# What is left of the earlier blocks in a layer's last step: done before or after the last block's scores

## The chip, the cores and the metric

The kernel runs on one core of one Trainium2 chip. The metric is the device time in microseconds (us) of one launch. Five engines work side by side, each through its own list of instructions: TensorE (PE in the profile; its weight loads are PEld), VectorE (DVE), ScalarE (ACT), GpSimd (POOL) and SyncE (SP), which here only issues transfers.

## The reference

Four layers of graph attention over the same 4096 nodes of 256 features. Each layer normalises x row by row, applies a relu, lets every node attend to its neighbours in `adj` (some eight of the 4096, and itself), and adds the result to x. Cut to what matters:

```python
# layers 0 to 2, with their own weights and slopes
h = relu(layernorm(x))
Wh = h @ W                                       # 4 heads of 64; one head of 256 in layer 1
e = leaky_relu(s_i[:, None] + s_j[None, :])      # s_i, s_j: one number a node and head
alpha = softmax(where(adj == 0, -inf, e), axis=1)
x = x + act(alpha @ Wh)                          # elu in layer 0; layer 1 returns Wh + alpha @ h
# layer 3
q, k, v = h @ Wq + bq, h @ Wk + bk, h @ Wv + bv  # 4 heads of 64
scores = q @ k.T / 8 + (adj.T - 1) * 10000
x = x + softmax(scores) @ v
```

## The kernel before

The first part of the kernel (some 400 us) turns `adj` into a list of neighbours for each node, sorts the nodes by their number of neighbours and writes them to DRAM in that order. It is not touched. After it the nodes lie in 32 blocks of 128, one node to a partition; a block needs as many gathers as its fullest node has neighbours (`CAPS`, 23 down to 3, and six fewer in layer 0). `ORDER` takes the blocks from both ends, 0, 31, 1, 30, and so on; the last four are 14, 17, 15 and 16, with 9, 8, 8 and 8 gathers. In the text they are w, x, y and z.

`layer(l)` (line 806 on) runs one layer. Each layer has a table in DRAM, one row to a node: its features, and the numbers its scores need; in layer 3 keys and values. A block goes through these stages:

- `fill`: GpSimd gathers one row per neighbour from the layer's table into `s_ring` (L755), up to four blocks ahead, as room in the ring allows. In layer 3 SyncE also loads the block's own values (L831).
- `scores`: VectorE and ScalarE work out the softmax's exponentials. In layers 0 to 2 these are small instructions over the gathered numbers (L912 to L945, the exp at L952). In layer 3 VectorE multiplies all gathered keys by the query and sums them (L932, L935, up to eight rows at a time), after a copy of the query by ScalarE (L927).
- `weigh`: VectorE divides by the sum (L987 to L989), multiplies the block's own row (L1014) and the gathered rows by their shares (L1028), and TensorE sums the rows in PSUM by matmuls with the identity (L1019, L1021, L1033, L1038).
- `settle`, in two parts: part 0 is ScalarE's exp for the elu, in layer 0 alone (L1052, L1053). Part 1 adds the sum to x and starts the next layer's normalisation (L1063 to L1067, statistics at L569 and L570, ScalarE at L575 and L577). In layer 3 it only makes the output block (L1057, L1058).
- `norm`: VectorE ends the normalisation (L579 to L585), ScalarE scales and applies the relu (L732), TensorE turns the block (L740). Empty in layer 3.
- `product`: ScalarE copies the turned block (L742), TensorE multiplies it by the next layer's weights (L748). Empty in layer 3.
- `third`: VectorE adds what is to be added to the product (L1080, or L1094 to L1104) and the row is sent to the next layer's table, by GpSimd after layer 0 (L765) and by SyncE after layers 1 and 2 (L1088, L1095). It also sends all that waits in `made`, in layer 3 the output blocks (L765).

Everything in the layers is issued in program order: an engine's list is what the Python loop writes. The loop is a pipeline over the blocks. With S = 2 and N = 3 (layers 0, 2 and 3) step i takes the scores and the weighing of block i, settles block i - 2, and does norm and product of block i - 3 and the third stage of block i - 4. Layer 1 has S = 0 and N = 1. After the last step a tail finishes what is left, by hand. The first gather of the next layer needs its whole table, so the last row that the tail writes.

In the profile DVE L1094 is thus third, L1067 settle, L579 norm, L932 or L913 the scores, L987 to L1028 weighing.

Of the kernel before, what the change touches and what calls it, by code (L numbers as in the profile page):

```python
# [50 lines left out]
ORDER = [b for k in range(16) for b in (k, 31 - k)]  # L51
# [18 lines left out]
class Sparse:  # L70
# [735 lines left out]
    def layer(self, l):  # L806


        nc, nt, vs = self.nc, self.nt, {}
        wide = (W, WL, W, 2 * D)[l]  # L810
        slots = RING // wide
        ring = self.ring[:, : slots * wide].rearrange("p (k w) -> p k w", w=wide)
        todo, held, at = list(ORDER), {}, 0
        made = []

        def fill(i):
            nonlocal at
            while todo and nt - len(todo) <= i + AHEAD:
                j = todo[0]
                K = self.slots(l, j)  # L820

                room = K + (K % 2 if l > 1 else 0)
                s = (at if at + room <= slots else 0) if K else 0
                if any(s < e and b < s + room for b, e in held.values()) or (
                    l == 3 and len(held) > 3
                ):
                    return
                todo.pop(0)
                if l == 3:
                    vs[j] = self.pool.tile([P, D], F32, name=f"s_vself_{j}", tag="vself", bufs=5)  # L830
                    nc.sync.dma_start(out=vs[j], in_=self.tab[3][ts(j, P), D:])  # L831
                k0 = EARLY if l == 0 else 0
                for k in range(K):
                    at_k = self.near[:, j, k0 + k : k0 + k + 1]
                    self.fetch(ring[:, s + k, :], self.tab[l], at_k)
                held[j] = (s, s + room)
                at = s + room if K else at

        sums, behind, turning, rows = {}, {}, {}, {}

        def settle(c, parts=(0, 1)):

            if 0 in parts and c in sums:
                behind[c] = self.settle(l, c, sums.pop(c), made)
                next(behind[c])
            if 1 in parts and c in behind:
                next(behind[c])

        def norm(d):

            if l < 3 and d in behind:
                turning[d] = self.turned(self.pool, next(behind.pop(d)), f"{l + 1}_{d}")
                next(turning[d])

        def product(d):
            if d in turning:
                rows[d] = self.advance(l + 1, d, next(turning.pop(d)), made)
                next(rows[d])

        def third(d):  # L860
            if d in rows:
                next(rows.pop(d), None)
            for send in made:
                self.send(*send)
            made.clear()

        S, N = (0, 1) if l == 1 else (2, 3)
        for i in range(nt):
            fill(i)
            b, c, d, e = (ORDER[k] if k >= 0 else None for k in (i, i - S, i - N, i - N - 1))  # L870
            if S:
                settle(c, (0,))
            norm(d)
            g = ring[:, held[b][0] : held[b][1], :]
            p = self.scores(l, b, self.rows[b], g[:, : self.slots(l, b), :])
            third(e)
            if S:
                settle(c, (1,))
            product(d)
            sums[b] = self.weigh(l, b, vs.pop(b) if l == 3 else self.rows[b][:, 0:D], g, p)  # L880
            del held[b]
            if not S:
                settle(b)
        z, y, x, w = ORDER[-1:-5:-1]
        if S:
            settle(y)
            norm(x)
            third(w)
            product(x)
            settle(z)  # L890
            norm(y)
            third(x)
            product(y)
        norm(z)
        third(y)
        product(z)
        third(z)

    def scores(self, l, b, mine, g):

# [775 lines left out]
```

## Time and profile before

| | us |
|---|---|
| median of three runs | 1838.98 (1837.8 to 1839.6) |
| span of the profiled execution | 1839.6 (1841.3 with what lies around it) |
| VectorE busy | 1379.9 (75%) |
| GpSimd busy | 1184.8 (64%) |
| TensorE busy, matmuls | 994.8 (54%) |
| ScalarE busy | 423.7 (23%) |
| first gather of layer 1, issued at | 658.8 |
| last table write of layer 2, issued at | 1409.6 |
| first gather of layer 3, issued at | 1412.4 |
| last output block, issued at | 1834.0 |

The profile is one execution. Its page gives each engine's busy time, the granted TensorE clock (mean 0.751 of full speed here), the chain that ended last, and groups of instructions; the trace behind it gives every instruction with its start, its duration and what ended the idle time before it. A busy share is a mean over stages with different limits, so a change at a layer's end is read in the timeline of that end.

### The profile page before, as it was taken

The page shows a single profiled execution, that of the slowest core. Times are in us where ns is not written, and L with a number is a line of the kernel's source. Part 1 is how long each engine was busy: PE and PEld are TensorE (multiplying, and loading weights), DVE is VectorE, ACT ScalarE, POOL GpSimd, SP SyncE. Part 2 cuts the span into 40 slices and gives each one's busy share as a digit, 9 for nine tenths or more (in the row PEclk, how much of TensorE's full clock was granted, in tenths as well). Part 3 has the DMA queues.
Part 4 walks back from the last instruction along what each step waited for, and adds up shares of the span by engine and source line. Part 5 has one row for each costly group of instructions (what it writes and reads, how often), then busy time and mean ns, then how long its engine had stood idle before and what let it go on. Part 6 is the DMA issues. An engine that isn't in the chain of part 4 may idle for free. (4 is left out here: it accounts for less than half of the span.)

```text
span 1839.6 us, 14362 instructions
## 1 busy us (share of the span) xinstructions
PE 994.8 (54%) x2569; PEld 481.7 (26%) x2569; DVE 1379.9 (75%) x3900; ACT 423.7 (23%) x1240; POOL 1184.8 (64%) x1324
## 2 busy tenths in 40 slices
PE   4878787750666611222232167788785344565555
PEld 3523232220455400111111023343342111221122
DVE  6899989850688808888888257888885587887777
ACT  5864435000244401111111002222222000000000
POOL 1067756676566357777776477777772577776774
PEclk9988889875788855555555588889987676777777
DMA  9899877348533134444444344444443577666763
GB/s 319 281 394 363 287 259 254 97 148 242 168 87 88 51 84 128 131 132 130 132 132 121 69 111 133 134 135 131 136 131 97 156 215 210 208 208 181 209 205 108
DMA packets 123017, 312.89 MB, mean 170 GB/s; under 512 B 31236, under 2 KB 49671, under 8 KB 122920
## 3 DMA queue, kind: packets, MB, share of 16 engines
q0 software_dynamic: 68064, 207.46, 39.7%
q1 hardware_dynamic: 54856, 104.44, 16.2%
q14 instruction: 73, 0.60, 0.1%
q8 instruction: 24, 0.39, 0.1%
HBM read 276.80 MB, written 35.00 MB: 169 GB/s over the span
## 5 line engine op out<-in xcount | busy, mean ns | idle before, releaser
L755 POOL DMA_INDIRECT s_ring<-s_tab,s_near x924 | 883.8, 956 | 356.7 <-issue 190.4
L1033 PE MATMUL s_acc<-s_ring,s_ident 128*128 128x512 f32 x588 | 319.5, 697 | 183.3 <-issue 95.0
L1033 PEld LDWEIGHTS s_acc<-s_ring,s_ident 128*128 128x128 f32 x588 | 130.5, 228 | 368.2 <-issue 245.5
L755 POOL DMA_INDIRECT s_g<-s_tab,s_keep x192 | 183.2, 954 | 64.3 <-issue 57.0
L483 DVE MAX8 s_cand<-s_pt 128x8 f32<-128x256 f32 x512 | 181.6, 417 | 16.4 <-PE s_pt L481 15.9
L1028 DVE TENSOR_TENSOR s_ring<-s_ring,s_shares 128x2048 f32<-128x2048 f32 (+7 forms) x121 | 187.5, 1573 | 0.0
L740 PE MATMUL s_pht<-s_ident,s_h 128*128 128x128 f32 x128 | 34.3, 361 | 248.0 <-ACT s_h L732 248.0
L748 PE MATMUL s_ps<-s_we_l,s_ht 128*128 128x264 f32 x256 | 113.4, 586 | 79.2 <-ACT s_ht L742 79.2
L999 DVE SCALAR_TENSOR_TENSOR s_acc<-s_ring,s_p,s_acc 128x256 f32<-128x256 f32 x277 | 135.7, 490 | 9.7
L261 ACT ACTIVATE s_low<-s_raw 128x1024 fp8e4<-128x1024 int32 x128 | 134.2, 1050 | 21.3 <-DMA s_raw<-in_adj_dram 18.1
L556 PE MATMUL s_ae<-s_g,s_ident 128*128 128x512 f32 x192 | 113.7, 688 | 36.5 <-DVE s_g L547 36.5
L913 DVE TENSOR_TENSOR s_e<-s_ring,s_rx 128x8 f32<-128x8 f32 (+12 forms) x87 | 15.7, 181 | 148.0 <-DMA s_ring<-s_tab,s_near 143.0
L476 PE MATMUL s_pt<-s_low,s_mark 128*128 128x512 fp8e4 x256 | 107.7, 421 | 34.3 <-DVE s_cand L483 15.0
L748 PE MATMUL s_ps_kv<-s_wkv,s_ht 128*128 128x512 f32 x128 | 82.9, 782 | 73.6 <-ACT s_ht L742 73.6
L932 DVE TENSOR_TENSOR s_ring<-s_ring,s_shares 128x2048 f32<-128x2048 f32 (+7 forms) x48 | 81.1, 1690 | 47.8 <-DMA s_ring<-s_tab,s_near 31.5
L481 PE MATMUL s_pt<-s_places,s_stands 128*128 128x512 bf16 x256 | 106.5, 416 | 1.4 <-DVE s_stands L453 1.4
L952 ACT ACTIVATE s_shares<-s_e 128x32 f32<-128x32 f32 (+8 forms) x87 | 17.4, 200 | 387.8 <-DVE s_e L945 340.2
L575 ACT ACTIVATE s_y<-s_mv,s_eps 128x1 f32<-128x1 f32 x96 | 28.3, 294 | 294.0 <-DVE s_mv L570 294.0
L740 PEld LDWEIGHTS s_pht<-s_ident,s_h 128*128 128x128 f32 x128 | 18.3, 172 | 287.9 <-ACT s_h L732 271.9
L748 PEld LDWEIGHTS s_ps<-s_we_l,s_ht 128*128 128x128 f32 x256 | 63.0, 272 | 110.0 <-ACT s_ht L742 100.1
L935 DVE TENSOR_REDUCE s_e<-s_ring 128x32 f32<-128x2048 f32 (+7 forms) x48 | 81.2, 1692 | 1.7
L1021 PE MATMUL s_acc<-s_me,s_ident 128*128 128x512 f32 x60 | 42.8, 803 | 70.8 <-DVE s_me L1014 67.2
(193 smaller groups left out, 1673.4 us busy)
## 6 DMA issues: line engine op xcount, KB each, us to landing
s_raw<-in_adj_dram SPq DMA_DIRECT2D x128, 512.0 KB, 7.8
s_ring<-s_tab,s_near POOLq DMA_INDIRECT x924, 3.0
s_rx<-s_placed SPq DMA_DIRECT2D x32, 262.0 KB, 8.0
s_tab<-s_kv SPq DMA_DIRECT2D x32, 256.0 KB, 2.8
s_tab<-s_keep SPq DMA_DIRECT2D x8, 528.0 KB, 6.8
s_tab<-s_rx SPq DMA_DIRECT2D x32, 132.0 KB, 2.3
s_keep<-in_x_dram SPq DMA_DIRECT2D x8, 512.0 KB, 4.1
s_vself<-s_tab SPq DMA_DIRECT2D x32, 128.0 KB, 2.9
```

What stands on the lines that cost most here:

```text
L261: nc.scalar.activation(low[r][:, ts(h, n // 4)], raw.pop(q), AF.Copy, saturate=False, accum_out=self.sums[:, r, h : h + 1],)
L476: nc.tensor.matmul(pt, lhsT=self.mark, rhs=lo[:, ts(g, IB)], start=True, stop=False)
L481: nc.tensor.matmul(pt, lhsT=self.stands[:, g, :], rhs=self.places, start=False, stop=True)
L483: nc.vector.max(out=cand[:, g * (IB // CH) + k, :], in_=pt[:, ts(k, CH)])
L556: nc.tensor.matmul(acc, lhsT=self.ident, rhs=g[:, :, k, 0:D], start=False, stop=(k == E - 1))
L748: self.nc.tensor.matmul(ps[:, :width], lhsT=ht[:, c, :], rhs=w[:, c, :], start=(c == 0), stop=(c == KC - 1),)
L755: return self.nc.gpsimd.indirect_dma_start(out=out, out_offset=None, in_=table[:, :], in_offset=bass.IndirectOffsetOnAxis(ap=idx, axis=0),)
L932: nc.vector.tensor_tensor(kq, kq, q.unsqueeze(1).to_broadcast([P, m, D]), ALU.mult)
L935: nc.vector.tensor_reduce(e[:, k0 : k0 + m, :], kq.rearrange("p k (h d) -> p k h d", h=4), AX.X, ALU.add)
L999: nc.vector.scalar_tensor_tensor(acc, g[:, k, 0:D], p[:, k, :], acc, ALU.mult, ALU.add)
L1028: nc.vector.tensor_tensor(v, v, p[:, k0 : k0 + m, :].unsqueeze(3).to_broadcast([P, m, H, D // H]), ALU.mult)
L1033: nc.tensor.matmul(both, lhsT=self.ident, rhs=g[:, k : k + 2, v0 : v0 + D], start=(k == 0 and not full), stop=(k + 2 >= K),)
```

## The change

In the last step of a layer with S = 2 (`final`), the order of the stages is written anew. Before, the step did part 0 of settle for x, norm(w), the scores of z, then third for the block before w, part 1 of settle for x, product(w), and the weighing of z; the tail did the rest: settle y, norm x, third w, product x, settle z, norm y, third x, product y, norm z, third y, product z, third z. After, part 1 of settle for x, the third stage, product(w), settle(y) and norm(x) are issued ahead of z's scores, and third(w), norm(y) and product(x) between z's scores and its weighing. The tail then has third x, product y, settle z, norm z, third y, product z, third z. No work is added or left out. In layer 1 the order is what it was.

```diff
@@ -868,33 +868,41 @@
             b, c, d, e = (ORDER[k] if k >= 0 else None for k in (i, i - S, i - N, i - N - 1))
+            final = S and i == nt - 1
+            y = ORDER[i - 1]
             if S:
                 settle(c, (0,))
             norm(d)
+            if final:
+
+                settle(c, (1,))
+                third(e)
+                product(d)
+                settle(y)
+                norm(c)
             g = ring[:, held[b][0] : held[b][1], :]
             p = self.scores(l, b, self.rows[b], g[:, : self.slots(l, b), :])
-            third(e)
-            if S:
-                settle(c, (1,))
-            product(d)
+            if final:
+                third(d)
+                norm(y)
+                product(c)
+            else:
+                third(e)
+                if S:
+                    settle(c, (1,))
+                product(d)
             sums[b] = self.weigh(l, b, vs.pop(b) if l == 3 else self.rows[b][:, 0:D], g, p)
...
-        z, y, x, w = ORDER[-1:-5:-1]
         if S:
-            settle(y)
-            norm(x)
-            third(w)
-            product(x)
-            settle(z)
-            norm(y)
-            third(x)
-            product(y)
-        norm(z)
+            third(c)
+            product(y)
+            settle(b)
+        norm(b)
         third(y)
-        product(z)
-        third(z)
+        product(b)
+        third(b)
```

## The prediction

> **What bounds the kernel now.** The page comes first: where does the change act? VectorE (DVE) is busy 75% of the span, GpSimd (POOL) 64%, mostly issuing gathers, TensorE (PE) 54%. No engine is full, so the change is priced where it sits: at the end of layers 0, 2 and 3 (layer 1 has S = 0, so `final` is false and its tail keeps its order). The waits view says what a layer's end costs:
>
> ```profile
> span 1839.6 us, 14362 instructions
> ...
> POOL s_ring L755 <- DMA s_vself<-s_tab: 33.6, 1, 33.6
> ...
> POOL s_ring L755 <- DMA s_tab<-s_rx: 22.5, 1, 22.5
> ```
>
> Between layers GpSimd stands still (once, 33.6 and 22.5 us), because the first gather of a layer needs the whole table, so the last block's row. What counts is thus when the last block z is done; at the very end, when its output is stored. I call the last four blocks w, x, y, z (z is `b` in the last step). Next the VectorE timeline of the three ends; in layer 3 (columns: start, duration, engine and line, idle before and its releaser):
>
> ```profile
> 1816.63 2.28 DVE L1028 TENSOR_TENSOR s_ring<-s_ring,s_shares 128x2048 f32<-128x2048 f32 x1
> 1819.41 2.29 DVE L932 TENSOR_TENSOR s_ring<-s_ring,s_shares 128x2048 f32<-128x2048 f32 x1 [0.50 <-ACT s_shares L927]
> ...
> 1824.60 0.22 DVE L945 TENSOR_TENSOR s_e<-s_e,s_m 128x36 f32<-128x36 f32 x1
> 1824.73 0.41 DVE L1057 TENSOR_TENSOR s_out<-s_rx,s_acc 128x256 f32<-128x256 f32 x1
> 1825.17 0.42 DVE L1058 TENSOR_TENSOR s_out<-s_out,s_acc 128x256 f32<-128x256 f32 x1
> 1825.51 0.19 DVE L987 TENSOR_REDUCE s_t<-s_shares 128x4 f32<-128x36 f32 x1
> ...
> 1828.92 0.41 DVE L1057 TENSOR_TENSOR s_out<-s_rx,s_acc 128x256 f32<-128x256 f32 x1
> 1829.37 0.42 DVE L1058 TENSOR_TENSOR s_out<-s_out,s_acc 128x256 f32<-128x256 f32 x1
> 1832.80 0.42 DVE L1057 TENSOR_TENSOR s_out<-s_rx,s_acc 128x256 f32<-128x256 f32 x1 [3.01 <-PE s_acc L1033]
> ```
>
> and TensorE in the same stretch:
>
> ```profile
> 1818.96 5.79 PE L1033 MATMUL s_acc<-s_ring,s_ident 128*128 128x512 f32 x8
> 1826.95 1.10 PE L1021 MATMUL s_acc<-s_me,s_ident 128*128 128x512 f32 x2 [2.20 <-DVE s_me L1014]
> 1829.06 3.70 PE L1033 MATMUL s_acc<-s_ring,s_ident 128*128 128x512 f32 x8 [1.01 <-DVE s_ring L1028]
> ```
>
> The reader is to see that VectorE does not wait for a gather here: it goes from y's weighing (L1028, to 1818.91) to z's scores (L932) with only half a microsecond between, while TensorE sums y's rows beside it. The pair of adds at 1828.92, y's, costs nothing: it lies under z's sum on TensorE.
>
> Layer 2's end is different. There z waits behind the others after its sum is ready:
>
> ```profile
> 1380.86 0.19 DVE L913 TENSOR_TENSOR s_e<-s_ring,s_rx 128x32 f32<-128x32 f32 x1 [1.24 <-DMA s_ring<-s_tab,s_near]
> ...
> 1395.15 0.87 DVE L1067 TENSOR_TENSOR s_rx<-s_rx,s_acc 128x256 f32<-128x256 f32 x2 [1.65 <-PE s_acc L1033]
> ...
> 1400.26 0.15 DVE L579 TENSOR_TENSOR s_y<-s_y 128x1 f32<-128x1 f32 x1
> ...
> 1402.85 0.69 DVE L1094 TENSOR_TENSOR s_kv<-s_ps_kv,s_bqkv 128x512 f32<-128x512 f32 x1 [1.85 <-PE s_ps_kv L748]
> ...
> 1408.92 0.69 DVE L1094 TENSOR_TENSOR s_kv<-s_ps_kv,s_bqkv 128x512 f32<-128x512 f32 x1 [3.55 <-PE s_ps_kv L748]
> ```
>
> z's sum is there at 1395.12, its norm (L579) only starts at 1400.26, its product is added at 1408.92.
>
> [...] the estimated end 1829.06 + 3.70 = 1832.76 is followed by the waiting add at 1832.80. [...] eight L1033 matmuls took 3.70 us after 2.2 us idle, 5.79 and 6.39 for y and x after longer gaps.
>
> **The change part by part.** It adds and removes no work, it moves it; each end is re-laid with the durations of this trace.
>
> *Layer 3.* norm and product are empty here, a settle is two adds.
> (1) x's adds move ahead of z's scores. x's sum is long there, its output buffer too (the store of three blocks earlier was issued at 1815.31, and the one before it, in the chain of waits, took 2.87 us to land). They run 1818.91 to 1819.8, over the 0.50 us wait for ScalarE's copy. Where they stood, between L945 and L987 (0.91 us start to start), the softmax's exp on ScalarE (1824.92 to 1825.12) appears: about 0.6 remains, a gain of 0.3.
> (2) settle(y) now stands ahead of z's scores, and VectorE must wait for y's sum: 1818.96 + 5.79 = 1824.75. That is a new wait of 5.0 us; behind it are queued all of z's scores, 5.4 us of VectorE work, and everything of z after them. y's adds end at 1824.79 + 0.88 = 1825.67. L932 starts there instead of 1819.41: +6.26. Their old place was free, so nothing returns. Net of (1): +5.95.
> (3) TensorE now idles from 1824.75 until z's first matmul at about 1826.95 + 5.95 = 1832.9, 8 us instead of 2.2. So z's eight matmuls run as those of the other blocks with eight neighbours did: 5.54, 5.37, 5.47, 5.92, 5.34, 6.39 and 5.79, mean 5.69, against 3.70: +2.0. Bounds 0 (full rate) and +2.7.
> (4) Stores: GpSimd's queue holds w's and x's store ahead of y's; stores follow at least 3.2 us apart (1815.31, 1818.48, 1821.68), so x at 1824.9, y at 1828.1, all before z's at about 1842. No cost.
> Layer 3: +8.0; ends +5.5 (y's sum as short as 5.34, z's at full rate) and +9.
>
> *Layer 2.* VectorE's pieces: settle part two 1.65 (1383.87 to 1385.52), norm 0.66, third 2.2, z's scores 1.0, weighing 3.4. New order from norm(w)'s end, 1379.46: settle x to 1381.1, third(v) to 1383.3, settle y (its sum is ready at 1383.31, no wait) to 1385.0, norm(x) to 1385.7, scores(z) to 1386.7 (the 1.24 us gather wait is covered), third(w) to 1388.9, norm(y) to 1389.5, weigh z to 1392.9 instead of 1388.9. On ScalarE y's relu follows w's squares, so y's transposes and x's products start at about 1390.9 on TensorE, as against w's at 1386.29; the products take 2.7 us at full rate (1376.17 to 1378.85) or 4.4 at the slow one (1386.29 to 1390.66), z's sum 4.46: ready at 1398.0 or 1399.7, i.e. +2.9 to +4.5, taken +3.5.
> After it: before, 13.8 us from z's sum to its L1094. Now settle 1.65, ScalarE's rstd 0.5, norm 0.75, relu 0.6, transposes 0.6 (y's products are over by then), then y's squares hold ScalarE to about +5.4, copy 0.35, products 2.0 to 3.0: 7.8 to 8.8. A gain of 5 to 6, taken 5.5: norm(y) and third(x) no longer stand ahead of norm(z), nor product(y) ahead of z's transposes. The SP queue's table writes keep their order, z's last.
> Layer 2: 3.5 - 5.5 = -2.0, ends -3.1 and -0.3.
>
> *Layer 0.* Here blocks are short (two or three gathered rows left) and VectorE is nearly full. settle y needs ScalarE's exp first, which stands behind product(w)'s copy: about 1.7 us of new VectorE wait at 637.8. New order: settle y to 641.2, norm(x), scores(z), third(w), norm(y) to 643.6, weighing to 645.4 instead of 640.3; z's sum, at the two TensorE rates, lets its exp start at 647.35 to 648.75 instead of 644.15: +3.2 to +4.6. From there to the store of z's row: 11.4 us before (644.15 to 655.55), now 7.7 to 8.6, as norm(y), third(x) and product(y) (649.01 to 651.13 on TensorE) are out of the way: -2.8 to -3.7.
> Layer 0: +0.7, ends -0.5 and +2.
>
> Sum: 0.7 - 2.0 + 8.0 = **+6.7**. The profiled execution has a span of 1839.6 (1841.3 with what lies around it) and becomes 1846.3; the median shown, 1838.98, is 0.6 below that span, so I forecast 1845.7.
>
> **The rivals.**
> B, not slower: [...] y's sum and z's run at full rate. Place: layer 3's end. Then y's sum ends at 1822.6, L932 moves by 3.8 net, z costs nothing; with the good ends of layers 0 and 2 (-0.5, -3.1) the sum is +0.2: 1839.2. It decides once the clock gives back 3 us of the 6.7. [...] Against: no block of eight but z ran its sum under 5.3 us late in the layer.
> C, slower still: the slow rate everywhere: +2, -0.3, +9, together +10.7: 1849.7. For it: layer 0's tail products already take 2.1 us, not 1.16.
> D, the change does not do what it says: instructions are not queued as written and the adds of y do not hold z's scores; only layers 0 and 2 count, -1.3: 1837.7. Against: every queue in these stretches follows the program's order.
>
> **How the numbers follow.** A 0.72, B 0.12, C 0.12, D 0.04. A's own range is about 1842.5 to 1848.5. Bounds of 2 to 3 us on three ends that need not err together, and the 1.8 us between the runs shown, give 1841.3 to 1849.7 for 8 in 10; it cuts B's centre and D off. 0.2% (3.7 us) is about what a measurement can tell from no change. Slower by more: C and nearly all of A, 0.80; within: B, half of D, a little of A, 0.16; faster: 0.04, which needs tails that gain twice what I found.
>
> **What would show it.** In layer 3 a VectorE wait of about 5 us for PE L1033 ahead of y's L1057, then L932; TensorE idle 8 us ahead of z's L1021; z's eight matmuls near 5.7 us. In layer 2 z's L579 within 3 us of its sum, and no L913 wait for a gather. It is wrong if y's add finds its sum ready, or if GpSimd's standstill between layers 2 and 3 shrinks by 5 us or more.

## The result, and the profile after

| | before | after |
|---|---|---|
| device time, median of 7 runs each | 1839.07 (1836.74 to 1840.61) | 1849.39 (1844.78 to 1850.49) |
| span of the profiled execution | 1839.6 | 1848.2 |
| mean granted TensorE clock | 0.751 | 0.746 |
| TensorE busy, matmuls | 994.8 | 1000.2 |

The changed kernel is slower: ratio 1.0051, 95% interval 1.0040 to 1.0063, or +9.4 us (+7.4 to +11.6) when worked out from the ratio; the two medians are 10.3 apart. 1845.7 was forecast. All engines do the same work as before: their busy times are within 1.2 us of those before, but for TensorE's, which is 5.4 us longer.

Lines of the layer code stand 8 higher after the change (L1028 is L1036, L932 is L940, L1057 is L1065, L1067 is L1075, L1094 is L1102). VectorE's timeline at layer 3's end, after (start, duration, engine and line, idle before and its releaser):

```profile
1818.76 2.28 DVE L1036 TENSOR_TENSOR s_ring<-s_ring,s_shares 128x2048 f32<-128x2048 f32 x1
1820.96 0.41 DVE L1065 TENSOR_TENSOR s_out<-s_rx,s_acc 128x256 f32<-128x256 f32 x1
...
1826.72 0.42 DVE L1065 TENSOR_TENSOR s_out<-s_rx,s_acc 128x256 f32<-128x256 f32 x1 [4.89 <-PE s_acc L1041]
...
1827.51 2.28 DVE L940 TENSOR_TENSOR s_ring<-s_ring,s_shares 128x2048 f32<-128x2048 f32 x1
...
1832.69 0.22 DVE L953 TENSOR_TENSOR s_e<-s_e,s_m 128x36 f32<-128x36 f32 x1
1833.24 0.20 DVE L995 TENSOR_REDUCE s_t<-s_shares 128x4 f32<-128x36 f32 x1 [0.33 <-ACT s_shares L960]
1841.40 0.42 DVE L1065 TENSOR_TENSOR s_out<-s_rx,s_acc 128x256 f32<-128x256 f32 x1 [4.66 <-PE s_acc L1041]
```

and TensorE's there:

```profile
1821.09 5.58 PE L1041 MATMUL s_acc<-s_ring,s_ident 128*128 128x512 f32 x8
1834.70 2.05 PE L1029 MATMUL s_acc<-s_me,s_ident 128*128 128x512 f32 x2 [8.02 <-DVE s_me L1022]
1836.80 4.57 PE L1041 MATMUL s_acc<-s_ring,s_ident 128*128 128x512 f32 x8
```

The new wait is the third line shown: y's add stands for 4.89 us at the head of VectorE's queue, with z's scores (L940) behind it. TensorE, which is to sum z's rows, has nothing to do for 8.02 us. From y's weighing (L1036) to z's first output add it is 22.64 us, where it was 1816.63 to 1832.80, 16.17: **+6.47**.

Layer 2's end after, VectorE from norm(w)'s last instruction on:

```profile
1379.91 0.16 DVE L585 SCALAR_TENSOR_TENSOR s_rn<-s_mv,s_rn 128x1 f32<-128x1 f32 x1
...
1385.57 0.88 DVE L1075 TENSOR_TENSOR s_rx<-s_rx,s_acc 128x256 f32<-128x256 f32 x2 [1.65 <-PE s_acc L1041]
...
1402.73 0.87 DVE L1075 TENSOR_TENSOR s_rx<-s_rx,s_acc 128x256 f32<-128x256 f32 x2 [2.62 <-PE s_acc L1041]
...
1404.88 0.16 DVE L579 TENSOR_TENSOR s_y<-s_y 128x1 f32<-128x1 f32 x1 [0.41 <-ACT s_y L577]
...
1411.94 0.69 DVE L1102 TENSOR_TENSOR s_kv<-s_ps_kv,s_bqkv 128x512 f32<-128x512 f32 x1 [4.13 <-PE s_ps_kv L748]
```

and TensorE there, first the product of the block before w, then x's product and z's sum:

```profile
1376.70 2.76 PE L748 MATMUL s_ps_kv<-s_wkv,s_ht 128*128 128x512 f32 x4 [2.27 <-ACT s_ht L742]
1379.25 1.91 PE L748 MATMUL s_ps_q<-s_w_q,s_ht 128*128 128x256 f32 x4
...
1392.61 0.69 PE L740 MATMUL s_pht<-s_ident,s_h 128*128 128x128 f32 x2 [3.33 <-ACT s_h L732]
1393.09 3.62 PE L748 MATMUL s_ps_kv<-s_wkv,s_ht 128*128 128x512 f32 x4
1396.50 1.90 PE L748 MATMUL s_ps_q<-s_w_q,s_ht 128*128 128x256 f32 x4
1398.21 1.05 PE L1029 MATMUL s_acc<-s_me,s_ident 128*128 128x512 f32 x2
1399.10 3.60 PE L1041 MATMUL s_acc<-s_ring,s_ident 128*128 128x512 f32 x8
```

z no longer queues behind the others: its norm (L579) follows its sum by 2.2 us instead of 5.1. But the sum itself is late. y's settle (the first L1075 shown) waited 1.65 us for TensorE, and x's product, which stands before z's sum on TensorE, ran at about half rate after a new gap of 3.33 us (3.62 and 1.90, where before it took 1.98 and 1.03). From L585 to z's L1102 it is 32.03 us; before, it is 29.54 from the following line to 1408.92: **+2.5**.

```profile
1379.38 0.16 DVE L585 SCALAR_TENSOR_TENSOR s_rn<-s_mv,s_rn 128x1 f32<-128x1 f32 x1
```

Layer 0's end after, VectorE:

```profile
634.31 0.16 DVE L585 SCALAR_TENSOR_TENSOR s_rn<-s_mv,s_rn 128x1 f32<-128x1 f32 x1
...
638.05 0.42 DVE L1071 SCALAR_TENSOR_TENSOR s_ex<-s_ex,s_rx 128x256 f32<-128x256 f32 x1 [1.59 <-ACT s_ex L1061]
...
648.60 0.42 DVE L1071 SCALAR_TENSOR_TENSOR s_ex<-s_ex,s_rx 128x256 f32<-128x256 f32 x1 [2.77 <-ACT s_ex L1061]
...
655.57 0.42 DVE L1088 TENSOR_TENSOR s_rx<-s_rx,s_ps 128x256 f32<-128x256 f32 x1 [3.74 <-PE s_ps L748]
```

The second line shown is settle(y) waiting for ScalarE's exp, the third is z's settle, the last z's row before it is sent. From norm(w)'s L585 to that last line it is 21.26 us. Before, the same two lines are 18.91 apart: **+2.35**.

```profile
635.63 0.16 DVE L585 SCALAR_TENSOR_TENSOR s_rn<-s_mv,s_rn 128x1 f32<-128x1 f32 x1
...
654.54 0.42 DVE L1080 TENSOR_TENSOR s_rx<-s_rx,s_ps 128x256 f32<-128x256 f32 x1 [2.87 <-PE s_ps L748]
```

The three make +11.3; all else drifted by -2.7 in this pair of executions (-1.3 ahead of layer 0's end, -0.5 from there to layer 2's, -0.9 from there to layer 3's), and the spans differ by 8.6. GpSimd's standstills say the same of layer 2; the waits view after:

```profile
POOL s_ring L755 <- DMA s_vself<-s_tab: 36.1, 1, 36.1
...
POOL s_ring L755 <- DMA s_tab<-s_rx: 22.5, 1, 22.5
```

33.6 became 36.1, longer, not shorter as a forecast of -2.0 for layer 2 would have it.

### The profile page after: what moved, and what is told of

The parts are those of the page before. It is cut to its first block, busy times and chain, and to the rows that moved or that the text cites. A ratio compares the mean times of both kernels' runs of the same rounds, so it can differ in the third digit from the quotient of the medians.

```text
span 1848.2 us, 14361 instructions
## 1 busy us (share of the span) xinstructions
PE 1000.2 (54%) x2569; PEld 484.0 (26%) x2569; DVE 1378.7 (75%) x3900; ACT 424.0 (23%) x1240; POOL 1183.8 (64%) x1324
## 5 line engine op out<-in xcount | busy, mean ns | idle before, releaser
L1036 DVE TENSOR_TENSOR s_ring<-s_ring,s_shares 128x2048 f32<-128x2048 f32 (+7 forms) x121 | 187.5, 1572 | 0.0
L940 DVE TENSOR_TENSOR s_ring<-s_ring,s_shares 128x2048 f32<-128x2048 f32 (+7 forms) x48 | 81.1, 1690 | 47.3 <-DMA s_ring<-s_tab,s_near 32.1
```

Of the source, the lines that this page charges most:

```text
L940: nc.vector.tensor_tensor(kq, kq, q.unsqueeze(1).to_broadcast([P, m, D]), ALU.mult)
L1036: nc.vector.tensor_tensor(v, v, p[:, k0 : k0 + m, :].unsqueeze(3).to_broadcast([P, m, H, D // H]), ALU.mult)
```

## The experiments

**Each layer's end alone.** The theory says that layer 3's new wait makes the loss; a rival, that it is spread over the three ends, or that layer 2 gives some back. Three kernels have the new order in one layer alone, the old step and tail in the others; this is the first, the second has `(2,)` and the third `(0,)`.

```diff
-            final = S and i == nt - 1
+            final = l in (3,) and i == nt - 1
```

> The new order in layer 3 alone, layers 0 and 2 as before. Theory (the loss is mostly the wait for y's sum at the end of layer 3): +6.5 us on the kernel before, with a VectorE wait of about 5 us for PE ahead of y's L1057-type add. Rival 1 (layers 0 and 2 gain or lose little on average, all of the loss is layer 3): +8 to +9. Rival 2 (the loss is made in layers 0 and 2): under +3.

> The new order in layer 2 alone. Theory as the trace of the changed kernel has it: +2.5 us on the kernel before, because z's sum comes some 7 us later and only 4.6 come back after it. Rival 1 (the prediction's sum, the traced loss being one execution's clock): -2.

> The new order in layer 0 alone. Theory: +2.3 us on the kernel before (z's exp 4.9 later, 2.6 back after it). Rival 1 (the prediction's sum): +0.7 or less.

The kernel before took 1839.66 beside them; the last column is worked out from the ratio, here and below.

| new order in | us | ratio (95%) | us more than before |
|---|---|---|---|
| layer 3 | 1846.09 | 1.0037 (1.0023 to 1.0051) | +6.8 (4.2 to 9.4) |
| layer 2 | 1838.96 | 0.9998 (0.9984 to 1.0012) | -0.4 (-2.9 to +2.2) |
| layer 0 | 1841.08 | 1.0011 (1.0001 to 1.0021) | +2.0 (0.2 to 3.9) |

Together +8.4, as much as the whole change within its interval. Layer 3 makes most of it, layer 0 some, and layer 2 gives back nothing that can be told from zero. The +2.5 that the one trace let expect for layer 2 lies outside its interval, the prediction's -2 inside. The runs alone leave some rivals: layer 3's interval reaches to +8 and +9, all of the loss, and layer 0's down to +0.7. VectorE at the end of the first (its lines stand 10 higher than after's):

```profile
1813.32 0.42 DVE L1076 TENSOR_TENSOR s_out<-s_out,s_acc 128x256 f32<-128x256 f32 x1
1819.53 0.42 DVE L1075 TENSOR_TENSOR s_out<-s_rx,s_acc 128x256 f32<-128x256 f32 x1 [5.79 <-PE s_acc L1051]
```

The wait is there again, 5.79 us: x's adds are done, y's sum is not ready. The stretch from y's weighing to z's first output add is 24.00 us in this trace, 7.8 longer than before.

**y's adds back behind z's weighing.** The whole change, but in layer 3 the one settle goes back into the tail. If the wait makes layer 3's loss, it goes; if x's earlier adds or a store made it, it stays.

```diff
-                settle(y)
+                if l < 3:
+                    settle(y)
...
         if S:
+            settle(y)
             third(c)
```

> The changed kernel with one thing undone: in layer 3 y's two adds go back behind z's weighing; x's adds stay ahead of z's scores, layers 0 and 2 keep the new order. Theory: 6 to 6.5 us faster than the changed kernel, so +3 to +5 on the kernel before, and TensorE idles about 2 us ahead of z's first matmul instead of 8. Rival 1: -1.3 on the kernel before. Rival 2: no more than 2 us faster than the changed kernel.

1840.33 against 1839.66 before: 1.0004 (0.9996 to 1.0012), +0.7 us. That is less than the +3 to +5 expected, which had layer 2 at +2.5; with the run's -0.4 for layer 2 and +2.0 for layer 0, +1.6 would be left, and that is inside the interval. VectorE at layer 3's end of this kernel:

```profile
1816.42 0.42 DVE L1068 TENSOR_TENSOR s_out<-s_out,s_acc 128x256 f32<-128x256 f32 x1
1816.76 2.28 DVE L942 TENSOR_TENSOR s_ring<-s_ring,s_shares 128x2048 f32<-128x2048 f32 x1
...
1829.79 0.42 DVE L1067 TENSOR_TENSOR s_out<-s_rx,s_acc 128x256 f32<-128x256 f32 x1 [3.00 <-PE s_acc L1043]
```

No wait stands between x's adds and z's scores, and the stretch from y's weighing to z's first output add is 16.02 us, 0.15 shorter than before the change. So the place of one `settle(y)`, two adds of 0.4 us, makes layer 3's whole loss.

The same kernel also has layer 2's new order, and there TensorE ran x's and z's products faster:

```profile
1389.39 3.31 PE L748 MATMUL s_ps_kv<-s_wkv,s_ht 128*128 128x512 f32 x4
1392.53 1.03 PE L748 MATMUL s_ps_q<-s_w_q,s_ht 128*128 128x256 f32 x4
...
1403.44 1.98 PE L748 MATMUL s_ps_kv<-s_wkv,s_ht 128*128 128x512 f32 x4 [1.54 <-ACT s_ht L742]
```

The first two lines are x's product, which took 3.62 and 1.90 after the change; the last is z's, 3.61 there. Layer 2's end took 27.55 us here, 32.03 there: one order, 4.5 us apart.

**TensorE kept busy over the gaps.** Part of the loss may be the clock: z's matmuls come after 8.02 us of nothing, and the granted clock under them was 0.71 (1834.7 to 1841.4), the eight taking 4.57 us. Before the change, with gaps of 2.20 and 1.01 us, it was 1.00 there (1826.9 to 1832.8) and they took 3.70. Extra matmuls of a weight with the identity, into a PSUM bank that is free there, fill the gap.

```diff
                 settle(y)
                 norm(c)
+                if l > 1:
+                    warm = self.pacc.tile([P, IB], F32, tag="acc", name=f"s_warm_{l}")
+                    for _ in range(7 if l == 2 else 16):
+                        nc.tensor.matmul(
+                            warm, lhsT=self.ident, rhs=self.wkv[:, 0, :], start=True, stop=True
+                        )
```

> The changed kernel with 7 (layer 2) and 16 (layer 3) extra matmuls into an unused PSUM bank, queued on TensorE behind x's transposes and so behind y's sum, to keep its clock up over the gaps ahead of x's product and of z's sum. Their results are not used. Clock theory (half of what the forecast missed is TensorE at half rate after the new gaps): x's product in layer 2 near 3.0 us instead of 5.5, z's eight matmuls in layer 3 at 3.7 us instead of 4.6 to 5.8; 2 to 4 us faster than the changed kernel, +5 to +7 on the kernel before. Rival (the waits alone matter): same as the changed kernel, +8 to +10, or slower where the extra matmuls stand in z's way.

1849.37 against 1838.58 before: 1.0057 (1.0043 to 1.0071), +10.5 us, no gain. TensorE at layer 3's end shows why:

```profile
1824.68 13.90 PE L886 MATMUL s_warm<-s_wkv,s_ident 128*128 128x512 f32 x32
...
1838.41 1.02 PE L1035 MATMUL s_acc<-s_me,s_ident 128*128 128x512 f32 x2
1839.27 3.60 PE L1047 MATMUL s_acc<-s_ring,s_ident 128*128 128x512 f32 x8
```

Sixteen calls are 32 matmuls of 0.43 us, 13.9 us for an 8 us gap, so z's own matmuls start late; but they run at full rate, 3.60 against 4.57. In layer 2 it is the same: x's product took 1.88 and 1.03, but its transposes began 2.5 us later behind the extra matmuls, and z's sum was ready only 0.3 us earlier. The number of calls was wrong, so the idea was tried again with 4 and 9 calls, beside the changed kernel.

> As the run with extra matmuls, but with 4 in layer 2 and 9 in layer 3: each is two passes of 0.43 us, so the first try filled 6.0 and 13.7 us where the gaps are 3.3 and 8.0; these fill 3.4 and 7.7. Their results are not used. Clock theory: x's product and z's sum at full rate and nothing delayed, 2 to 4 us faster than the changed kernel. Rival (the waits alone matter): within 1 us of the changed kernel.

> The changed kernel itself, beside the run with fitted extra matmuls on the same chip: +7 to +11 on the kernel before under every theory; in its profile the end of layer 2, from norm(w)'s L585 to z's third stage, is 27.5 us if TensorE happens to be at full rate there and about 32 if not.

The chip that ran these two took 2174.5 us for the kernel before itself, with runs from 2164 to 2185. Ratios there: 1.0028 (1.0012 to 1.0044) with the extra matmuls, 1.0021 (1.0005 to 1.0038), +4.6 us, for the changed kernel. By the runs they can't be told apart. By the two traces the extra matmuls shortened layer 2's end to 27.81 from 30.34 us (x's product took 1.97 and 1.03 instead of 3.62 and 1.91) and layer 3's to 21.97 from 22.94. The 30.34 is neither of the two lengths that were expected. Both were run once more on a chip with the usual times.

> The run with fitted extra matmuls again, since the one before fell on a chip on which the kernel before took 2174.5 us and the runs lay 20 us apart. Clock theory: 2 to 4 us faster than the changed kernel. Rival: within 1 us of it.

> The changed kernel beside the run with fitted extra matmuls: +7 to +11 on the kernel before.

With the extra matmuls 1846.21 (1844.67 to 1846.94), 1.0042 (1.0028 to 1.0056), +7.7; without, 1848.2 (1846.2 to 1848.87), 1.0052 (1.0038 to 1.0065), +9.6. TensorE at layer 3's end with them:

```profile
1822.08 7.89 PE L886 MATMUL s_warm<-s_wkv,s_ident 128*128 128x512 f32 x18
1830.26 1.10 PE L1035 MATMUL s_acc<-s_me,s_ident 128*128 128x512 f32 x2 [0.29 <-DVE s_me L1028]
1832.37 3.70 PE L1047 MATMUL s_acc<-s_ring,s_ident 128*128 128x512 f32 x8 [1.01 <-DVE s_ring L1042]
```

and without, on the same chip:

```profile
1830.42 2.05 PE L1029 MATMUL s_acc<-s_me,s_ident 128*128 128x512 f32 x2 [8.02 <-DVE s_me L1022]
1832.52 5.12 PE L1041 MATMUL s_acc<-s_ring,s_ident 128*128 128x512 f32 x8
```

When z's matmuls can start is still set by VectorE; only their rate changes, 3.70 for 5.12. The stretch at layer 3's end is 21.76 instead of 24.29, but only 1.4 of these 2.5 us are z's matmuls: 1.1 is y's wait, 4.87 instead of 5.99, and that ends before the extra matmuls have run. In layer 2 nothing was to be gained in this pair, as x's product ran at full rate in both (1.97 and 1.03; the ends took 29.28 and 29.49). So the traces put the part of layer 3's loss that is TensorE's rate under z's sum at 1.0 to 1.4 us. How much of the wait itself is its rate stays open: y's sum, which ends the wait, took 5.6 to 6.7 us in every execution of this order, and no run sped it up. The times don't show it on their own: the medians are 2.0 apart, but the intervals of the two ratios overlap, and two of the five runs of the changed kernel lie within the range of the other.

**The tail's part alone.** The change does two things: it moves the others' work ahead of z's scores, and it takes it out from between z's sum and z's row. The second can be had without the first: the last step as before (but for x's adds in layer 3, which go behind z's weighing), and a tail in which z is served as soon as its sum is there. That needs one more PSUM bank for products, taken from the sums; a control has only this, the first four lines of the diff. (In the diff several calls stand on one line, and layer 1's tail, which stays as it was, is not shown.)

```diff
-            self.pacc = ctx.enter_context(tc.tile_pool(name="s_pacc", bufs=4, space=PSUM))
+            self.pacc = ctx.enter_context(tc.tile_pool(name="s_pacc", bufs=3, space=PSUM))
-            self.pp = ctx.enter_context(tc.tile_pool(name="s_pp", bufs=3, space=PSUM))
+            self.pp = ctx.enter_context(tc.tile_pool(name="s_pp", bufs=4, space=PSUM))
...
+            if l == 3:
+                settle(x, (1,))
             settle(y); norm(x); third(w); product(x)
-            settle(z); norm(y); third(x); product(y)
-        norm(z); third(y); product(z); third(z)
+            settle(z, (0,)); norm(y)
+            if l == 0:
+                product(y)
+            settle(z, (1,)); norm(z); third(x)
+            if l == 2:
+                product(y)
+            product(z); third(y); third(z)
```

> The kernel before with its last step as it was (z's scores and weighing first), only the tail rewritten: z's settle and norm come ahead of third(x), product z ahead of third(y), norm y in the wait for z's sum; in layer 3 x's adds move behind z's weighing; one PSUM bank goes from the sums to the products so that this is possible. Theory (what the change wins is in the tail, what it loses is work put ahead of z's scores): 3 to 6 us faster than the kernel before, layer 2's end shorter by 3, layer 0's by 2, layer 3's by 0.4. Rival (the tail's order is hidden by the gathers or by TensorE's rate): within 1.5 us of the kernel before.

> The kernel before with only the PSUM banks of the layers divided 3 and 4 instead of 4 and 3. Both theories: within 1.5 us of the kernel before; it is the control for the run with the new tail.

The new tail: 1837.02, 0.9987 (0.9978 to 0.9995), -2.4 us (-4.0 to -0.9). The banks alone: 1838.76, 1.0000 (0.9991 to 1.0008). The gain is smaller than the 3 to 6 us expected. In layer 0, which was to give 2 of them, nothing was gained: z's product was added 16.36 us after norm(w)'s L585 instead of 18.91, but layer 1's first gather came 23.03 us after it, and 23.14 before. GpSimd's sends there, with the new tail:

```profile
647.04 0.97 POOL L765 DMA_INDIRECT s_tab<-s_rx,s_near  x1 [4.24 <-ACT s_rx L1092]
...
650.27 0.97 POOL L765 DMA_INDIRECT s_tab<-s_rx,s_near  x1 [2.25 <-issue]
...
653.49 0.97 POOL L765 DMA_INDIRECT s_tab<-s_rx,s_near  x1 [2.25 <-issue]
```

Three rows' sends, x's, y's and z's, follow one another 3.22 us apart, though z's row was ready 2.7 us before it was sent, and the first of them waited for `third(x)`, which now stands behind norm(z). So in layer 0 it goes ahead of it:

```diff
+            if l == 0:
+                third(x)
             norm(z)
-            third(x)
+            if l > 0:
+                third(x)
```

> The kernel with the new tail, with one more move: in layer 0 third(x) goes ahead of norm(z), into the 0.4 us in which VectorE waits for ScalarE. In the run with the new tail the three last stores of layer 0's rows followed one another at 3.22 us (647.04, 650.27, 653.49)[...], while z's row was ready some 2.5 us before its store. Theory: x's store goes out 1.5 us earlier and z's with it; 3 to 5 us faster than the kernel before. Rival: no gain over the new tail alone, 1 to 4 us faster than the kernel before.

1833.98, 0.9978 (0.9970 to 0.9986), -4.1 us (-5.5 to -2.6): faster than the kernel before and the changed one. That the move adds to the new tail's -2.4 is not shown by the runs, whose intervals overlap; the traces show it. GpSimd's sends now:

```profile
644.19 0.97 POOL L765 DMA_INDIRECT s_tab<-s_rx,s_near  x1 [2.94 <-ACT s_rx L1095]
...
647.41 0.97 POOL L765 DMA_INDIRECT s_tab<-s_rx,s_near  x1 [2.25 <-issue]
...
650.62 0.97 POOL L765 DMA_INDIRECT s_tab<-s_rx,s_near  x1 [2.25 <-issue]
653.85 1.00 POOL L755 DMA_INDIRECT s_ring<-s_tab,s_near  x1 [2.26 <-DMA s_tab<-s_rx,s_near]
```

Counted from norm(w)'s L585 in each trace, the first send starts 1.3 us earlier, 12.06 instead of 13.35 (the rest of the 2.9 us between the two prints was there before layer 0's end), and the row of three keeps its spacing, so layer 1's first gather comes at 21.72 instead of 23.03. At layer 2's end both traces are shorter than any of the old order, 26.0 and 24.8 us against 26.9 to 29.5, and at layer 3's they are 15.8 against 16.2.

## Why the prediction was right, and where its sizes were off

**Layer 3, (1) to (4).** The steps hold. The new wait was put at 5.0 us and took 4.89 (5.08, 5.79 and 5.99 in three other executions of this order). VectorE did not let z's scores pass the waiting add: they stood behind it for its 4.89 us, and no longer did once the two adds were moved back. L940 moved by 5.97, after taking off 2.13 by which the layer's end came later as a whole; 6.26 was forecast, and y's sum took 5.58 instead of the 5.79 it was worked with. The x adds' gain was put at 0.3 and measures 0.36 (L953 to L995 is 0.55 instead of 0.91). The stores cost nothing: y's was issued at 1830.18, z's at 1842.56. TensorE's gap was put at 8 us and is 8.02. That a gap of this length would slow z's matmuls was the author's estimate, from the sums of the other blocks, and they were slower. But term (3) was too big: z's eight matmuls took 4.57, so +0.9, and 5.02, 5.12 and 4.66 in three other executions of this order, +1.0 to +1.4, where +2.0 was taken. The mean of the earlier blocks, 5.69, was the wrong measure for z. Four of its seven rows (5.54, 5.37, 5.47, 5.92) are not blocks with eight neighbours but with seven, their own row being the eighth: no pair of L1021 matmuls goes ahead there, while in z this pair took the first slow 2.05 us. Why the other three (5.34, 6.39, 5.79) were longer than z's stays open. Forecast +8.0, measured +6.5 in the profiled pair and +6.8 by run. The three other executions of this order have +6.8, +7.8 and +8.1, the last two with the longer waits, so the sum was nearer than its terms: a term that was too big stood in for a wait that can be a microsecond longer.

**Layer 2.** Here the sign is not shown: -2.0 was forecast, and it is -0.4 (-2.9 to +2.2) by run and +2.5 in the profiled pair. In that pair two terms failed. First, z's sum was ready 7.05 us later than before, once an upstream 0.53 is off, and not 3.5 (2.9 to 4.5). Of this, 1.7 is that settle(y) did not find its sum ready: it waited 1.65 us, as the product of the block before w, ahead of that sum on TensorE, took 2.76 and 1.91 instead of 1.98 and 1.03. This product is queued before the step that the change rewrites, and in three of the five executions of this order it ran fast and settle(y) had no wait, as forecast. The 1.24 us wait for z's gather did go. The rest, beyond the 2.9 worked out for TensorE's full rate, is x's product: it took from 1393.09 to 1398.21, 5.1 us, where 2.7 to 4.4 was allowed. Second, what follows the sum shrank from 13.8 to 9.24 us, where 7.8 to 8.8 was worked out, a gain of 4.6 instead of 5.5; z's product at the slow rate is the difference. (By its own terms the upper end of this layer was 4.5 - 5.0 = -0.5, not -0.3.) So the mechanism was seen, and the gap that it opens on TensorE was priced in layer 3 and too low here.

The five executions of the new order differ in just these three places. The gap ahead of x's transposes was 3.33 us in each, and x's product then took 5.1 us in three of them, 4.0 in one and 2.7 in one. The wait of settle(y) was there in two. z's product took 1.98 for its first four matmuls in one and 3.6 to 3.8 in four. The 27.55 us are no wait, 4.0 and 1.98, the 32.03 are 1.65, 5.1 and 3.61. What sets the rate each time stays open. In layer 3 the shortest and the longest gaps agree: after 0.29 and 1.06 us of idling z's first two matmuls took 1.10, after 8.02 they took 2.04 or 2.05. In between, the length of the gap alone does not decide, as the three results after 3.33 us show. It is the same for y's first two matmuls in layer 3: they took 2.04 or 2.05 after 2.72 to 2.96 us of idling in four traces, and 1.10 to 1.14 after 3.76 to 3.90 in four others. In three of the first four the sum ahead of the gap had taken 6.34 to 6.42 us, in the others 5.33 to 5.40, so TensorE may have been slow before the gap already.

A further fault is that one execution's 29.54 was taken for the old order: four traces with the old order in this layer gave 26.87, 29.06, 29.45 and 29.54 (mean 28.7), five of the new 27.55, 29.49, 30.32, 30.34 (this one from the slower chip) and 32.03 (mean 29.9). A term of -2 can't be read from one trace where the stretch itself scatters by 3 to 4.5 us within one order.

**Layer 0.** +0.7 was forecast, within -0.5 to +2; measured +2.0 (0.2 to 3.9) by run, and in the traces the new order's stretch is 21.25 to 21.27 us (four executions; 20.19 on the slower chip), the old one's 18.85 to 19.15 (four), +2.1 to +2.4. VectorE's part was right: the wait for the exp was put at 1.7 and took 1.59, and the weighing ended 4.96 later where 5.1 was worked out. TensorE's was not: x's product (1.97 us, against 1.16 at full rate) and z's sum (1.68, against 1.10) were slow, so z's exp came at 647.73, which is 4.9 later (644.15, less 1.32 of upstream shift; 3.2 to 4.6 was forecast), and from it to the send it took 8.84 us (7.7 to 8.6 forecast), with 3.60 us of TensorE idle ahead of z's transposes and a product of 2.13. Both terms came out a little beyond their slow ends. C, the slow rate everywhere, had +2 for this layer, and here that is what happened.

**The whole.** +6.7 forecast and +9.4 measured: layers 0 and 2 were each some 1.5 us too low by run, layer 3 1.2 too high, and 1.0 remains between the sum of the three runs and the whole. 1849.39 lies above A's own range (1842.5 to 1848.5), just under the top of the stated one, and next to C's 1849.7. C is not borne out as a whole: the slow rate came in layer 0 and mostly in layer 2, but z's sum in layer 3 was never as slow as C has it. So direction and main place were foreseen, and the size came out within the range in part because layer 3's excess made up for some of what the other two lacked. B, in which the clock gives back 3 us of layer 3's loss, was the author's estimate, and is excluded by the runs: that loss was there in every profiled execution of this order, and z's matmuls were slow in each that had no extra ones. D is excluded by the waits shown.

Open is also how the new tail's gain divides over the layers by run, as it was not tried in one layer at a time; the traces have most of it at layer 2's end.

## What to carry to other kernels

Work moved ahead of the last block's critical work in an engine's list is only free if its inputs are there when its turn comes; look up when they are ready, because a short add that waits can hold up what stands behind it and idle the engine that was to come next: here a wait of 4.89 us, with the adds, moved z's scores by 5.97 and left TensorE idle for 8.02. What delays the last block between its own stages is better moved behind it than ahead of its first stage. Before a term of a microsecond or two is put in a sum, see how far the same stretch scatters between traces, and price TensorE's slow rate at every gap of a few us that the change opens, not only at the largest: after 3.33 us x's product took 4.0 or 5.1 us instead of 2.7 in four of five executions.

## What the runs showed of the hardware

- A matmul call of 128x512 in f32 stood as two records of 0.43 us each at the faster rate: 16 calls are "x32" and took 13.9 us.
- GpSimd's indirect stores that stood ready followed each other 3.17 to 3.23 us apart: 0.97 for the issue and some 2.2 of standing. Mostly the trace names no releaser for that; in some lines it is the landing of the store before (2.23), and layer 1's first gather stands as long for the last store (2.26). Where several rows ended together, as in layer 0 with the new tail (sends at 647.04, 650.27 and 653.49, layer 1's first gather at 656.72), this spacing and not the last row's arithmetic set the end.
- Matmuls that do nothing useful kept TensorE's rate up over an 8 us gap: z's eight took 3.70 us instead of 4.66 and 5.12 in the two pairs of traces. Where they overran the gap (13.9 us), nothing was gained.
- After one and the same idle gap of 3.33 us a product took 2.7, 4.0 or 5.1 us in different executions.
- One chip ran the same kernel in 2174.5 us instead of 1839. In the changed kernel GpSimd's two standstills between layers took 70.7 and 80.6 us there instead of 22.5 and 36.1. The bytes are the same, so the mean of 143 GB/s instead of 169 only says that the span is longer; the cause stays open.
